# A two-layer attention kernel: loads and means in a new order at its beginning, scores, sums and check in a new order at its end

## The chip, the core and the metric

The kernel runs on one core of a Trainium2 chip. The metric is device time in microseconds (us) from launch to end. The profile names the engines PE (TensorE, matrix products), PEld (its weight loads), DVE (VectorE), ACT (ScalarE), POOL (GpSimd) and SP (SyncE, which issues DMAs); a q behind a name means the engine's sequencer, which waits, branches or issues. L348 is line 348 of the kernel before.

## What is computed

Sixteen images of 256 channels and 32 x 32 positions go through the same layer twice, with other weights each time:

```python
xn = gn(x)                      # 16 groups of 2 columns of h; mean and variance over channels, w and the 2 columns
q, k, v = Wq@xn + bq, Wk@xn + bk, Wv@xn + bv        # 4 heads of 64 channels, n = 1024 positions
rel = (rel_h + rel_w).reshape(heads, d, n)
attn = softmax(q^T k + rel^T q, axis=-1)            # n x n for each head
x = x + v @ attn^T
```

All is float32.

## The kernel before

**Units and blocks.** A unit is one image in one layer; there are 32, and `units` orders them so that an image's second layer comes some units after its first. A unit has two pairs of heads, a pair two halves of 512 output positions; each such half is a block, numbered 0 to 127. A block works over eight groups j of 128 positions of the softmax axis.

**A block.** For each j, `seed` (L327) has VectorE write the position term of the scores into a PSUM tile, as a broadcast sum of two small tables that `positions` (L297) has multiplied out. `scores` (L342) adds the product of k and q to it: four products of 64 x 64 weights and 512 columns, one for each quarter of the array (two row halves are the two heads, two column halves the two parts of j). ACT takes the exponential with a constant shift (L357), and `add_up` (L360) adds the eight results up on VectorE for the softmax sums. `attend` (L372) multiplies the eight results with v. It does so in two stretches, `values_of_p(0)` and `values_of_p(1)`, since the second writes the same PSUM places from the other half of the array's rows: `stretches` (L143) has GpSimd set a one-element tile, `token` (L152), when the first stretch is done, and the second waits for it. The products q, k and v of the next unit, its normalisation and its position tables are spread over the blocks (`prepare`, L472, and the `norm_` functions), and stand on TensorE between the scores. The last unit's blocks 126 and 127 have no such pieces.

**The softmax sums.** In the second block of a pair `sums_of_p` (L395) multiplies the added-up results of both blocks with ones and writes them beside the attention output in the same PSUM tile. `take_out` (L412) has ACT copy both out, and four DMAs lay the sums out over the partitions of `den_all`. Two blocks later `reciprocals` (L435) inverts them (a 128 x 16 form), sends them to DRAM and reads them back broadcast; `finish` (L450) multiplies, adds bias and the image, and in the second layer sends the result out. For the last pair these two steps follow block 127 (L714, L715).

**The check.** The constant shift is right only while all sums lie in a range. After the fast path the kernel compares all 1024 columns of `den_all` with both bounds (L969, L971), takes the minimum (L973), sums it over the partitions with a product (L975) and writes the count to `flag` (L977). All engines read the flag and branch round a slower general path (L979), which these inputs don't take.

**PSUM and order.** The eight banks of PSUM are four tiles of two banks, named a, b, c and d; `ring` says which block step uses which. The order of every engine's work is the order in the source (`manual_schedule`); an engine takes its instructions in that order.

**The beginning.** Lines 603 to 610 issue the loads: image 0, Wq and Wk of layer 0, the small tables of layer 0 (eleven DMAs of positions tables and biases, `load_rest`, L925, on ACT's queue), both Wv, image 1, Wq and Wk of layer 1, image 2, and the tables of layer 1. Eight semaphores serve all DMAs in turn, so a later DMA waits for the landing of an earlier one. `transposed` (L113) turns the weights on TensorE and has ACT copy them out of PSUM. Unit 0 is normalised by special code: `reduced` (L620) sums on VectorE, `first_mean` (L631) averages over partitions with a product, ACT and VectorE share squares and centring, `first_var` (L647) makes variance, reciprocal square root (GpSimd's power, L652) and shift (L654), ACT normalises 5 groups from x and VectorE scales 11. Then come q, k, positions and values of unit 0, and beside them unit 1's centring, squares and variance, on VectorE and GpSimd.

Of the kernel before, what the change touches and what calls it, by code (L numbers as in the profile page):

```python
# [17 lines left out]
P = 128  # L18
# [25 lines left out]
def flat(ap):  # L44
    return ap.rearrange("p w h -> p (w h)")
# [7 lines left out]
def fast_path(ctx, tc, sh, x, layers, out, W, den_all, token):  # L53
# [58 lines left out]

    def transposed(tag, raw, parts):  # L113
        ps = psum2(tag, raw.name + "_t")
        for a in range(2):
            for cc in range(CC):
                for oc in range(CC):
                    nc.tensor.transpose(
                        ps[:, a, cc * C + oc * P : cc * C + (oc + 1) * P],
                        raw[:, a, oc * C + cc * P : oc * C + (cc + 1) * P],  # L120
                        W.ident,
                    )
        for a, (l, part) in enumerate(parts):
            w = {"Wq": W.wq, "Wk": W.wk, "Wv": W.wv}[part][l]
            nc.scalar.copy(w.rearrange("p a c -> p (a c)"), ps[:, a, :])
# [9 lines left out]
    def psum2(tag, name):  # L135
        return ps_s.tile([P, 2, HALF], F32, tag=tag, name=name)
# [205 lines left out]
    def scores(blk, j):  # L342
        u, pr, half = blk
        ps = seeds.pop((blk, j))
        for h, hs in enumerate(QUARTERS):
            for x, c in enumerate(QUARTERS):
                j0 = j * P + x * D
                nc.tensor.matmul(  # L348
                    ps[c, h, :],
                    ks[u, pr][hs, j0 : j0 + D],  # L350
                    qs[u, pr][hs, half * HALF : (half + 1) * HALF],
                    start=False,
                    stop=True,
                    skip_group_check=True,
                )
        p = ppool.tile([P, 2, HALF], F32, tag="p", name=f"p_{u}_{pr}_{half}_{j}")
        nc.scalar.activation(p, ps, AF.Exp, bias=W.shift)  # L357
        probs[blk, j] = p
# [53 lines left out]
    def take_out(blk, po):  # L412

        u, pr, half = blk
        if half == 0:
            outs[u, pr] = opool.tile([P, 3, HALF], F32, tag="od", name=f"od_{u}_{pr}")
            nc.scalar.copy(
                outs[u, pr][:, 0, :].rearrange("p (a n) -> p a n", a=2), po[:, :, :QUART]
            )
            return  # L420
        od = outs[u, pr]
        nc.scalar.copy(  # L422
            od[:, 1:3, :].rearrange("p z (a n) -> p z a n", a=2),
            po.rearrange("p a (z n) -> p z a n", z=2),
        )
        R = P // 4
        n = index[blk]
        for x in range(2):
            for h in range(2):
                r0 = (2 * x + h) * R  # L430
                nc.sync.dma_start(  # L431
                    den_all[h * D : (h + 1) * D, n - 1 + x, :], od[r0 : r0 + 1, 2, :]
                )

    def reciprocals(u, pr):  # L435

        n = index[u, pr, 0]
        r8 = fpool.tile([P, 2, 8], F32, tag="r8", name=f"r8_{u}_{pr}")
        nc.vector.reciprocal(r8, den_all[:, n : n + 2, :])
        rd = dpool.tile([2, 2, HALF], F32, tag="rd", name=f"rd_{u}_{pr}")  # L440
        for x in range(2):
            nc.sync.dma_start(rd[:, x, :].rearrange("h (a b) -> h a b", b=8), r8[:, x, :])
        rdens[u, pr] = opool.tile([P, 2, HALF], F32, tag="rden", name=f"rden_{u}_{pr}")
        for h in range(2):
            nc.sync.dma_start(
                rdens[u, pr][h * D : (h + 1) * D],
                rd[h : h + 1].to_broadcast([D, 2, HALF]),
            )
# [12 lines left out]

    blocks = [(u, pr, half) for u in range(NU) for pr in range(CC) for half in range(NH)]
# [3 lines left out]

    ring = ["b", "c", "a", "d"]
# [30 lines left out]
    def block(n):  # L498
# [7 lines left out]
        pieces = u + 1 < NU or b < 2  # L506
        f0, f1, f2, f3 = ring

# [38 lines left out]
        if pieces and half == 0:  # L547
            ring[2:] = f3, f2
# [52 lines left out]


    load_x(0)
    raw0 = load_raw("raw0", [(0, "Wq"), (0, "Wk")])
    W.load_rest(nc.scalar, 0)
    raw1 = load_raw("raw1", [(0, "Wv"), (1, "Wv")])
    load_x(1)
    raw2 = load_raw("raw2", [(1, "Wq"), (1, "Wk")])
    load_x(2)
# [10 lines left out]
    def reduced(u):  # L620
        red = small.tile([P, CC, G], F32, tag="first_red", name=f"first_red_{u}")
        for cc in range(CC):
            nc.vector.tensor_reduce(
                red[:, cc, :],
                xt[units[u][0]][:, cc, :].rearrange("p (w g t) -> p g w t", g=G, t=GT),
                AX.XY,
                ALU.add,
            )
        return red

    def first_mean(u, pm, red):  # L631
# [15 lines left out]
    def first_var(u, pm, red):  # L647
        nc.tensor.matmul(pm, W.avg, red, start=True, stop=True)
        var = small.tile([P, G], F32, tag="var", name=f"var_{u}")
        nc.vector.tensor_scalar(var, pm, EPS, None, ALU.add)  # L650
        rstd = small.tile([P, G], F32, tag="rstd", name=f"rstd_{u}")
        nc.gpsimd.tensor_tensor(rstd, var, W.mhalf[:, :G], ALU.pow)  # L652
        shift = small.tile([P, G], F32, tag="nshift", name=f"nshift_{u}")
        nc.gpsimd.tensor_tensor(shift, negs[u], rstd, ALU.mult)  # L654
        rss[u] = (rstd, shift)

    G1, G2 = G // 2 + 1, G // 4 + 1
    transposed("a", *raw0)
    transposed("b", *raw1)
    pm0 = psum2("c", "pm_0")  # L660
    first_mean(0, pm0[:, 0, :G], reduced(0))
    norm_squares(0, range(G1))
    centred(0, G1, G)
    sq = ppool.tile([P, 2, HALF], F32, tag="p", name="first_sq_0")
    sq = sq.rearrange("p a n -> p (a n)")[:, : CC * sh.W * (G - G1) * GT].rearrange(
        "p (w g t) -> p w g t", g=G - G1, t=GT
    )
    nc.vector.tensor_tensor(sq, by_group(xns[0], G1), by_group(xns[0], G1), ALU.mult)
    nc.vector.tensor_reduce(
        sums[0][:, G1:], sq.rearrange("p w g t -> p g w t"), AX.XY, ALU.add  # L670
    )
    first_var(0, pm0[:, 1, :G], sums.pop(0))
    transposed("a", *raw2)
    pm1 = psum2("d", "pm_1")
    first_mean(1, pm1[:, 0, :G], reduced(1))
    centred(0, G2, G1)
    norm_apply(0, range(G2))
    nc.vector.tensor_tensor(
        by_group(xns[0], G2), by_group(xns[0], G2), spread(rss[0][0], G2), ALU.mult
    )  # L680
# [9 lines left out]
    centred(1, 0, G)  # L690
    red = small.tile([P, CC, G], F32, tag="first_red", name="first_sums_1")
    for cc in range(CC):
        sq = ppool.tile([P, 2, HALF], F32, tag="p", name=f"first_sq_1{cc}")
        sq = sq.rearrange("p a n -> p (a n)")
        nc.vector.tensor_tensor(sq, xns[1][:, cc, :], xns[1][:, cc, :], ALU.mult)
        nc.vector.tensor_reduce(
            red[:, cc, :], sq.rearrange("p (w g t) -> p g w t", g=G, t=GT), AX.XY, ALU.add
        )
    nc.vector.tensor_tensor(sums[1], red[:, 0, :], red[:, 1, :], ALU.add)
# [3 lines left out]
    first_var(1, pm1[:, 1, :G], sums.pop(1))  # L703
# [7 lines left out]
    seed(blocks[0], 3, ring[0])  # L711
    for n in range(len(blocks)):
        block(n)
    reciprocals(*blocks[-1][:2])  # L714
    finish(*blocks[-1][:2])  # L715

# [226 lines left out]
def kernel(  # L943
# [12 lines left out]
    token = const.tile([1, 1], F32, tag="token", name="token")  # L956
    with tc.manual_schedule():
        W = Weights(tc, sh, layers, const)
        fast_path(tc, sh, x, layers, out, W, den_all, token)


    with ExitStack() as s:
        pool = s.enter_context(tc.tile_pool(name="chk", bufs=1))
        psum = s.enter_context(
            tc.tile_pool(name="chk_ps", bufs=1, space=bass.MemoryType.PSUM)
        )
        flatden = den_all.rearrange("p n e -> p (n e)")
        low = pool.tile([P, nblk * 8], F32, tag="low", name="low")
        nc.vector.tensor_scalar(low, flatden, DEN_LO, None, ALU.is_ge)  # L969
        good = pool.tile([P, nblk * 8], F32, tag="good", name="good")  # L970
        nc.vector.scalar_tensor_tensor(good, flatden, DEN_HI, low, ALU.is_le, ALU.mult)  # L971
        cnt = pool.tile([P, 1], F32, tag="cnt", name="cnt")
        nc.vector.tensor_reduce(cnt, good, AX.X, ALU.min)  # L973
        pc = psum.tile([P, 1], F32, tag="pc", name="pc")
        nc.tensor.matmul(pc[0:1, :], cnt, W.ones[:, 0:1], start=True, stop=True)  # L975
        flag = const.tile([1, 1], I32, tag="flag", name="flag")
        nc.vector.tensor_copy(flag, pc[0:1, :])  # L977
# [33 lines left out]
```

## Time and profile before

| what | value |
|---|---|
| median of 3 runs | 2645.45 us (2643.64 to 2645.61) |
| profiled execution, its own time | 2646.91 us |
| span, first to last instruction | 2643.5 us |
| mean granted TensorE clock | 0.994 |
| busy: PE, PEld, DVE, ACT, POOL | 2589.6, 1394.9, 2422.9, 1979.9, 175.3 us |
| L348, one pass of a score product, 64x512 | 593 ns, 8192 of them |
| L332, one seed, 128x1024 | 1228 ns, 1024 of them |
| L357, one exponential, 128x1024 | 1114 ns |
| L652, GpSimd's power at the beginning | 2.9 us |
| first q product (L251) | starts at 25.91 us |
| last attention product to flag | 2615.2 to 2637.9 us |

A float32 product runs as two passes, and the four quarters of the array work at the same time: the passes of one score group start within 20 ns of each other and the next group's 429 ns later, so a group of four products holds TensorE for 0.86 us. [...] A group of the timeline is a row of start, length, engine, line, operation and count; the rows of the chain are start, length and what; those of the windows give for each engine the busy time and the number of its instructions, then the granted clock (PEclk), the share of the DMA engines and GB/s.

### The profile page before, as it was taken

What the parts mean: (1) busy time and instruction counts of PE and PEld (TensorE: products, weight loads), DVE (VectorE), ACT (ScalarE), POOL (GpSimd) and SP (SyncE); (2) the same over time, 40 slices, a digit from 0 to 9 for tenths busy, and PEclk for the clock granted to TensorE, in tenths of its full rate; (3) what the DMA queues carried; (4) which work ended last, traced back from release to release, by engine and by line L of the source; (5) the groups of instructions that cost most, each with busy time, mean ns of one, the idle gap of its engine ahead of it and who ended that gap; (6) DMA issues with size and microseconds to landing.
All of it is one profiled execution on the core that took longest, in us unless ns stands there. A gap on an engine that the chain in (4) does not pass through costs nothing.

```text
span 2643.5 us, 86127 instructions
## 1 busy us (share of the span) xinstructions
PE 2589.6 (98%) x38406; PEld 1394.9 (53%) x38406; DVE 2422.9 (92%) x2198; ACT 1979.9 (75%) x3916; POOL 175.3 (7%) x450
## 2 busy tenths in 40 slices
PE   7999999999999999999999999999999999999994
PEld 3555555555555555555555555555555555555552
DVE  6999999999999999999999999999999999999996
ACT  5787777787777887777877777877778777778652
POOL 1000000000000000000000000000000000000000
PEclk9999999999999999999999999999999999999997
DMA  2010010100101010010100101001010100100001
GB/s 75 11 34 19 10 50 18 34 26 18 42 19 41 19 42 18 18 50 10 42 26 10 50 18 34 27 16 44 19 34 26 36 25 18 30 14 27 26 26 34
DMA packets 61499, 75.48 MB, mean 29 GB/s; under 512 B 43200, under 2 KB 44736, under 8 KB 61120
## 3 DMA queue, kind: packets, MB, share of 16 engines
q1 hardware_dynamic: 59664, 69.83, 9.0%
q8 instruction: 302, 4.95, 0.8%
q14 instruction: 77, 0.63, 0.1%
q10 hardware_dynamic: 1456, 0.07, 0.0%
HBM read 52.04 MB, written 17.30 MB: 26 GB/s over the span
## 4 chain that ended last, share of the span: by engine, by line
PE 96%; issue 1%; DVE 1%; DMA 1%; POOL 0%; ACT 0%; SPq 0%; DVEq 0%; POOLq 0%
PE po L382 34%; PE ps L348 33%; PE pk L251 8%; PE pv L281 8%; PE pq L251 8%; PE po L405 2%; PE pa L309 2%; PE pm L196 0%; DMA den_all<-od 0%; DVE ps L332 0%; SPq L431 0%; POOL rstd L652 0%; DVE acc L368 0%; ACT od L422 0%; DMA rden<-rd 0%
## 5 line engine op out<-in xcount | busy, mean ns | idle before, releaser
L332 DVE TENSOR_TENSOR ps<-abt 128x1024 f32<-128x1024 f32 x1024 | 1228.7, 1228 | 121.6 <-ACT p L357 103.8
L357 ACT ACTIVATE p<-ps,shift 128x1024 f32<-128x1024 f32 x1024 | 1091.7, 1114 | 325.9 <-PE ps L348 203.8
L348 PE MATMUL ps<-q,k 64*64 64x512 f32 x8192 | 995.5, 593 | 7.4 <-DVE ps L332 7.1
L368 DVE TENSOR_TENSOR acc<-acc,p 128x1024 f32<-128x1024 f32 x768 | 933.6, 1216 | 16.5 <-ACT var L218 0.5
L382 PE MATMUL po<-p,v 64*64 64x256 f32 x16384 | 934.2, 377 | 0.3 <-POOL token L152 0.3
L382 PEld LDWEIGHTS po<-p,v 64*64 64x64 f32 x16384 | 670.0, 133 | 294.6 <-issue 60.9
L348 PEld LDWEIGHTS ps<-q,k 64*64 64x64 f32 x8192 | 301.7, 133 | 427.6 <-issue 281.5
L251 PE MATMUL pq<-xn,Wq 64*64 64x512 f32 x2048 | 244.6, 593 | 4.0 <-ACT xn L231 4.0
L281 PE MATMUL pv<-Wv,xn 64*64 64x256 f32 x4096 | 244.3, 376 | 1.5 <-POOL token L152 1.3
L251 PE MATMUL pk<-xn,Wk 64*64 64x512 f32 x2048 | 244.0, 592 | 0.0
L231 ACT ACTIVATE xn<-x,nshift,rstd 128x128 f32<-128x128 f32 x501 | 213.5, 500 | 1.6 <-POOL nshift L654 1.6
L281 PEld LDWEIGHTS pv<-Wv,xn 64*64 64x64 f32 x4096 | 153.8, 133 | 103.0 <-issue 52.1
L176 ACT ACTIVATE junk<-x,neg 128x128 f32<-128x128 f32 x489 | 191.6, 400 | 0.0
L152 POOL MEMSET token<- 1x1 f32 x380 | 33.5, 88 | 2351.3 <-PE po L382 660.9
L422 ACT COPY od<-po 128x1024 f32<-128x1024 f32 x64 | 64.8, 1012 | 152.2 <-PE po L405 152.2
L366 DVE TENSOR_TENSOR acc<-p,p 128x1024 f32<-128x1024 f32 x128 | 155.9, 1218 | 0.0
L251 PEld LDWEIGHTS pq<-xn,Wq 64*64 64x64 f32 x2048 | 78.6, 134 | 145.7 <-issue 133.1
L176 ACT ACTIVATE junk<-x 128x128 f32<-128x128 f32 x480 | 145.1, 312 | 0.8 <-DVE x L457 0.8
L251 PEld LDWEIGHTS pk<-xn,Wk 64*64 64x64 f32 x2048 | 75.8, 134 | 125.0 <-issue 125.0
L220 POOL TENSOR_TENSOR rstd<-var,mhalf 128x16 f32<-128x16 f32 x30 | 112.3, 3743 | 59.2 <-ACT var L218 59.2
L262 ACT ACTIVATE q<-pq,bq 128x1024 f32<-128x1024 f32 x64 | 71.4, 1116 | 39.4 <-PE pq L251 39.4
L291 ACT COPY v<-pv 128x1024 f32<-128x1024 f32 x64 | 64.8, 1012 | 48.1 <-PE pv L281 48.1
(59 smaller groups left out, 929.2 us busy)
## 6 DMA issues: line engine op xcount, KB each, us to landing
rden<-rd SPq DMA_DIRECT2D x128, 256.0 KB
x<-in_x_dram SPq DMA_DIRECT2D x32, 512.0 KB
out_dram<-x SPq DMA_DIRECT2D x32, 512.0 KB
den_all<-od SPq DMA_DIRECT2D x256, 2.0 KB
rd<-r SPq DMA_DIRECT2D x128, 4.0 KB
raw<-in_L_conv_Wq_dram SPq DMA_DIRECT2D x2, 256.0 KB
raw<-in_L_conv_Wk_dram SPq DMA_DIRECT2D x2, 256.0 KB
raw<-in_L_conv_Wv_dram SPq DMA_DIRECT2D x2, 256.0 KB
```

The costliest lines, as they stand in the source:

```text
L176: nc.scalar.activation(junk, grouped(xt[units[u][0]], g), func, accum_out=into[:, g : g + 1], **bias)
L220: nc.gpsimd.tensor_tensor(rstd, var, W.mhalf[:, :G], ALU.pow)
L231: nc.scalar.activation(grouped(xns[u], g), grouped(xt[units[u][0]], g), AF.Identity, bias=shift[:, g : g + 1], scale=rstd[:, g : g + 1],)
L251: yield nc.tensor.matmul(pk[c, nh, :], w[l][rs, cc, c0 : c0 + D], xns[u][rs, cc, nh * HALF : (nh + 1) * HALF], start=(t == 0 and cc == 0), ...
L262: nc.scalar.activation(t.rearrange("p (a n) -> p a n", a=NH), pk, AF.Identity, bias=bias[l][:, pr : pr + 1])
L281: yield nc.tensor.matmul(pv[c, a, i, :], xns[u][rs, cc, j0 : j0 + D], W.wv[l][rs, cc, :], start=(t == 0 and cc == 0 and i == 0), stop=(t = ...
L332: nc.vector.tensor_tensor(ps.rearrange("p h (w y) -> p h w y", y=H), ab[:, :, :H].unsqueeze(2).to_broadcast([P, 2, XH, H]), ab[:, :, H + h ...
L348: nc.tensor.matmul(ps[c, h, :], ks[u, pr][hs, j0 : j0 + D], qs[u, pr][hs, half * HALF : (half + 1) * HALF], start=False, stop=True, skip_g ...
L357: nc.scalar.activation(p, ps, AF.Exp, bias=W.shift)
L366: nc.vector.tensor_tensor(accs[blk], probs[blk, 0], probs[blk, 1], ALU.add)
L368: nc.vector.tensor_tensor(accs[blk], accs[blk], probs[blk, j], ALU.add)
L382: yield nc.tensor.matmul(po[c, a, :QUART], vts[u][rs, j, c0 : c0 + D], p[rs, h, a * QUART : (a + 1) * QUART], start=(t == 0 and j == 0), s ...
```

## The change

It has two parts, and one change in between.

**Beginning.** The loads come in the order image 0, Wq and Wk of layer 0, image 1, both Wv, Wq and Wk of layer 1, tables of layer 0, image 2, tables of layer 1, all on SP's queue. The means of unit 0 stand ahead of the weight transposes, and those of unit 1 ahead of q. The copies of transposed weights are split off (`taken`). ACT squares 10 groups of unit 0 and VectorE 6; VectorE centres all 16 groups, and both engines scale the centred copy (ACT 4 groups, VectorE 12), so unit 0 has no shift. ACT squares half of unit 1's groups. Unit 1's power comes behind the first values, and its shift is made on VectorE.

**Scores.** In `scores` the loop over the column halves is now outside and that over the row halves inside, for every block.

**End.** Blocks 126 and 127 have a function of their own. Scores 4, 5 and 6 of both have no seed: the position term is a second product, of q with a wide table that VectorE makes in block 125 (`widen`). Seed 7 comes ahead of the others. Block 126's sums are taken in block 127 after scores 3, and their reciprocals are fetched in it. Block 127's sums go to PSUM tiles of their own: as rows that are already spread over the partitions, whose reciprocal VectorE takes directly (128 x 512), and as columns for the check. The last image is finished and sent in halves. The check of the first 992 columns of `den_all` stands in block 126, that of the rest at the end.

```diff
-    W.load_rest(nc.scalar, 0)
+    load_x(1)
     raw1 = load_raw("raw1", [(0, "Wv"), (1, "Wv")])
-    load_x(1)
     raw2 = load_raw("raw2", [(1, "Wq"), (1, "Wk")])
+    W.load_rest(nc.sync, 0)
     load_x(2)
...
+    G1, G2 = G // 2 + 2, G // 4
+    pm0 = psum2("c", "pm_0")
+    for cc in range(CC):
+        reduced(0, cc)
+    first_mean(0, pm0[:, 0, :G])
     transposed("a", *raw0)
+    norm_squares(0, range(G1))
+    centred(0, 0, G)
+    rest_of_squares(0, G1)
+    rstd0 = first_rstd(0, first_var(0, pm0[:, 1, :G]))
+    taken(raw0[1])
     transposed("b", *raw1)
+    taken(raw1[1])
+    pm1 = psum2("d", "pm_1")
+    for cc in range(CC):
+        reduced(1, cc)
+    first_mean(1, pm1[:, 0, :G])
+    transposed("a", *raw2)
+    for g in range(G2):
+        nc.scalar.activation(
+            grouped(xns[0], g), grouped(xns[0], g), AF.Identity, scale=rstd0[:, g : g + 1]
+        )
+    nc.vector.tensor_tensor(
+        by_group(xns[0], G2), by_group(xns[0], G2), spread(rstd0, G2), ALU.mult
+    )
+    taken(raw2[1])
+    norm_squares(1, range(0, G // 2))
+    centred(1, G // 2, G)
+    rest_of_squares(1, G // 2)
...
     seed(blocks[0], 3, ring[0])
+    rstd1 = first_rstd(1, var1)
+    shift1 = small.tile([P, G], F32, tag="nshift", name="nshift_1")
+    nc.vector.tensor_tensor(shift1, negs.pop(1), rstd1, ALU.mult)
+    rss[1] = (rstd1, shift1)
     for n in range(len(blocks)):
         block(n)
-    reciprocals(*blocks[-1][:2])
-    finish(*blocks[-1][:2])
```

```diff
-        for h, hs in enumerate(QUARTERS):
-            for x, c in enumerate(QUARTERS):
+        for x, c in enumerate(QUARTERS):
+            for h, hs in enumerate(QUARTERS):
                 j0 = j * P + x * D
...
+                terms = [(ks[u, pr], qs[u, pr])]
+                if tag:
+                    terms = [(qs[u, pr], wide[u, pr])] + terms
+                for i, (a, b) in enumerate(terms):
...
+    def block_without_pieces(n, half):
+
+        blk = blocks[n]
+        u, pr, _ = blk
+        f0, f1, f2, f3 = ring
+        if half == 1:
+            add_up(blocks[n - 1], 7)
+        for j in range(1, 4):
+            scores(blk, j)
+        if half == 1:
+            po = pos[n - 1]
+            sums_of_p(blocks[n - 1 : n], po)
+            nc.scalar.copy(
+                outs[u, pr][:D, 2, :].rearrange("p (a n) -> p a n", a=2), po[:D, :, QUART:]
+            )
+            keep_sums(outs[u, pr], n - 1, 1)
+        add_up(blk, 1)
+        seed(blk, 7, f2)
+        add_up(blk, 2)
+        reciprocals(*(blocks[n - 2][:2] if half == 0 else (u, pr, 1)))
+        add_up(blk, 3)
+        for j, tag in ((4, f1), (5, f0), (6, f1)):
+            scores(blk, j, tag)
+        scores(blk, 7)
+        add_up(blk, 4)
+        if half == 0:
+            seed(blocks[n + 1], 0, f0)
+        po = pos[n] = psum2(f3, f"po_{n}")
+        values_of_p = attend(blk, po)
+        values_of_p(0)
+        if half == 0:
+            scores(blocks[n + 1], 0)
+        if half == 0:
+            seed(blocks[n + 1], 1, f1)
+            seed(blocks[n + 1], 2, f2)
+        add_up(blk, 5)
+        if half == 0:
+            seed(blocks[n + 1], 3, f0)
+        add_up(blk, 6)
+        if half == 0:
+            finish(*blocks[n - 2][:2])
+            in_range(flatden[:, : 8 * (n - 2)], 0)
+            values_of_p(1)
+            take_out(blk, po)
+            return
+        add_up(blk, 7)
+        acc = accs.pop(blk)
+        pd = psum2(f0, "pd")
+        sums_on_rows(acc, pd)
+        values_of_p(1)
+        finish_half(u, pr, 0, outs[u, pr][:, 0, :], rdens[u, pr][:, 0, :])
+        rden = rdens[u, pr][:, 1, :]
+        nc.vector.reciprocal(rden, pd[:, 0, :])
+        pd = psum2(f2, "pd_columns")[:, 0, : 2 * HALF // P]
+        sums_on_columns(acc, pd)
+        finish_half(u, pr, 1, po[:, :, :QUART], rden)
+        in_range(flatden[:, 8 * (n - 3) : 8 * n], 1)
+        in_range(pd, 2)
+        nc.vector.tensor_reduce(good[:, 3:4], good[:, 0:3], AX.X, ALU.min)
+        pc = psum2(f1, "pc")[0:1, 0, 0:1]
+        nc.tensor.matmul(pc, good[:, 3:4], W.ones[:, 0:1], start=True, stop=True)
+        nc.vector.tensor_copy(flag, pc)
```

`finish_half` is `finish` on 512 columns, `in_range` the two comparisons and the minimum, `sums_on_rows` two products of 64 columns of ones with 512 columns of sums, `sums_on_columns` eight products with 128 columns of sums as weights and one column of ones. `W.load_rest`, `sums_of_p`, `attend` and `seed` are as before.

## The prediction

> **What bounds the kernel now.** I read the chain that ended last first, then its first 70 us and its last 80 us in order of time, then the timeline of both stretches, the windows with the granted clock, and the row of the reciprocal.
>
> ```profile
> PE 96%; issue 1%; DVE 1%; DMA 1%; POOL 0%; ACT 0%; SPq 0%; DVEq 0%; POOLq 0%
> ```
>
> TensorE carries 96% of the span. The rest lies at the two ends. At the beginning:
>
> ```profile
> 19.12 2.92 POOL rstd L652
> ...
> 22.11 1.67 POOL nshift L654
> ...
> 25.91 3.69 PE pq L251 x16
> ...
> 40.38 1.17 POOL nshift L654
> 41.55 0.04 POOL token L152
> ...
> 41.64 1.96 PE pv L281 x32
> ```
>
> The columns are start, length, what. The first real product, q, starts at 25.91, after GpSimd's power and shift. At 40.38 GpSimd is busy with unit 1's shift while TensorE waits for a one-element memset in the same queue. From 41.64 to about 2577 TensorE doesn't stop. At the end:
>
> ```profile
> 2615.20 1.04 PE po L405 x16
> ...
> 2624.87 3.93 DMA rden<-rd
> ...
> 2631.50 2.65 DMA out_dram<-x
> ...
> 2637.78 0.15 DVE flag L977
> ```
>
> The last attention product ends at 2615.2; 22.7 us of sums, DMA round trips, finish, output and check follow until the flag at 2637.9, and a fixed 5.5 us of branch and barriers to 2643.5.
>
> ```profile
> 2581.50:2584.90 3.40, 1.01 (x8) 0.21 (x8) 3.40 (x5) 0.88 (x1) 0.00 (x0) 1.00 0.04 2
> 2584.90:2588.30 3.40, 2.22 (x16) 0.75 (x16) 3.40 (x5) 1.21 (x2) 0.00 (x0) 0.50 0.58 154
> ```
>
> In the last two blocks VectorE is full (3.40 of 3.40) and TensorE busy 1.01: the seeds bound them, and after that stretch the granted clock is 0.50 until 2591.7.
>
> **The beginning, step by step.** Image 0's second half lands at 5.76; its reduce ends at 7.0 now too. Today L633 stands behind 16 weight transposes, so the negative mean comes at 14.55. Afterwards the means are first: 0.71 from reduce to ACT (as 21.28 to 21.99 for unit 1) plus 0.20 gives 7.9. The ACT table load (1.28, now at 8.47 behind eleven small DMA issues) becomes ACT's first instruction and hides under the load of x. Then ACT squares 10 groups at 0.39 (3.59 for 9): 11.9. VectorE centres all 16 groups (2.31, row of the 128x2048 form), squares and sums 6 groups: 768 elements at the slope between 680 ns for 512 and 1091 ns for 896 are 0.96 each. It ends at 12.25, and is the later. Product and variance as now (18.17 to 19.03) 0.86: 13.1. Power on GpSimd with its start 3.0: 16.1. The shift (1.67) leaves the path, because the centred copy is only scaled: VectorE scales 12 groups, 1536 elements, in 1.76: 17.9. ACT's four groups wait for unit 1's mean: VectorE reduces unit 1 in 2.33 behind the variance (15.45), 0.71 to ACT, 0.2, four groups 1.65: 18.0. TensorE does the third pair of transposes behind that mean: 2.0, to 18.15. So three engines meet at 18.1, and q starts at 18.15 instead of 25.91: **7.75 us**.
>
> Moved on SP: image 1 ahead of Wv, and eleven small tables from ACT's queue to SP's, ahead of image 2 and layer 1's tables. In the trace a DMA waits for the semaphore of an earlier one (Wq is issued at 4.33, when x lands); the changed program's first eight loads have none. About 3.5 MB at the 350 to 400 GB/s of the busy microseconds is 9 to 10 us: weights by about 13, needed at 12.9 (Wv) and 16.1. The tables, 0.6 us an issue, land by about 17; q's bias is first read near 26, rel near 28. Image 2 lands near 21 instead of 19, first read about 37. All this costs nothing under the chain above; if Wv were 2 us late, ACT's copies would push its scaling by about as much.
>
> Unit 1's shift goes to VectorE, and its power behind the token. q, k, positions and values keep their lengths (q start to first scores), but the second stretch of values starts when scores 0 end, 40.2 instead of 41.64: **1.45 us**. The power's reader, the first normalisation in block 0, comes seven microseconds later. The clock: q's weight loads step 0.85 us until 31.7 and 0.43 after, so TensorE ran at half for 5.8 us. The Trainium skill ("TensorE: Matmul & The Clock Gate", Part 1) has a free-running window of 3.4 us that must be busy, which makes this 3.4 to 6.8, less if the transposes that now run up to q count. Half of the difference is the gain: -0.5 to 2.9; I take **0.7**. Beginning: 9.9, from 8 to 12.
>
> **The middle.** `scores` now loops over columns outside and rows inside, in all 1024 groups of four products. No row has this order. A changed order next to products in the old one could cost one or two dispatch slots, the 6.5 ns by which the four starts of a group lie apart, at some ten changes in each of 126 blocks: 8 to 16 us, and the skill's Part 3 of that page says so: matmuls start and end strictly in program order.
>
> ```profile
> 1002.94 0.65 PE L348 MATMUL ps<-q,k 64*64 64x512 f32 x2
> 1002.95 0.21 PE L196 MATMUL pm<-sum,avg 64*64 64x16 f32 x2
> 1003.01 1.05 PE L348 MATMUL ps<-q,k 64*64 64x512 f32 x6
> ```
>
> But here a pair of scores starts before the second pass of the mean that stands ahead of it, and the other pair 0.07 later: each quarter of the array follows its own queue. By the rule 8 to 16 us, by the row **0**, both ends: the four start within 20 ns and stream 429 ns, and the last in either order is the same quarter, so nothing is gained. I take 0.
>
> **The end.** `widen` (one 1.22 us add) enters block 125 ahead of a seed that ended 0.48 before TensorE took it: VectorE is back to back there, the seed comes 1.02 late, TensorE stalls **0.6**. Block 126: six seeds in two blocks are replaced by a second term of the scores, 0.86 us of TensorE each, saving 1.13 of VectorE. Times without the 0.6: scores 1 to 3 end 2579.1; 4, 5, 6 at 1.72 and 7 at 0.86: 2585.1 (their exps, 1.11, are done in time); values 3.45, score 0.86, values 3.45: 2592.9, where before it was 2598.4. VectorE in the meantime: from 2578.8 three adds and seed 7, reciprocal, four seeds, two adds (1.13 unchained, 1.26 chained) to 2593.1, then finish 2.5, the check of 992 old sums 3.1 (0.70 + 1.23 + 1.22 now), the last add 1.2: 2599.8. Queued on TensorE behind that add are the sums of block 126, and behind them block 127's scores 4: TensorE is done with scores 3 at 2595.5 and **waits 4.3 us**. The windows above say what follows: 2.4 us idle in one brought half clock for 6.8 us. I charge 1.8 (0.8 of about 2.2).
>
> Then: sums 1.05, copy 0.6, two DMAs 2.35: reciprocal at 2604.0 (VectorE waits 0.75); five chained adds to 2610.6; TensorE's scores 4 to 7 and values, 9.5 us, end 2610.4. Sums on rows 0.95, values 3.5: 2615.15. Half 0's reciprocals arrive by DMA (6.9 after 2604.25) at 2611.2, its finish takes 1.35. Then a reciprocal of 512 elements.
>
> ```profile
> L439 DVE RECIPROCAL r<-den_all x64: 252/253/255, 88.7 to 2621.0; 128x16 f32<-128x16 f32 x64
> ```
>
> A 16-element scalar op takes 173 ns, of which 156 are fixed; the reciprocal 253, so 6.1 ns an element: 512 make 3.3 us. The skill ("VectorE: DVE Perf Modes", "First, the fixed hardware budget") says the divide repeats 8 times, at 0.96 GHz 8.3 ns: 4.4; and if the extra were fixed, 0.75. I take the row's 3.3: 2615.95, so it ends behind the values and is on the path. Finish of half 1 1.35; two small checks (3 ops of 0.2 each) and the minimum 1.45; product and flag 0.55: 2619.3. The eight column sums (16 weight loads of 0.11 to 0.21) end before the second check. The output's 2.65 lies beside this and the 5.5 us of the exit, where SP collects the DMA semaphores. With 0.6 and 1.8 the flag comes at 2621.7 instead of 2637.9: **16.2**, from 13.5 to 19.5.
>
> **Sum.** 9.9 + 16.2 = 26.1. The profiled execution had 2643.5 of span in 2646.9; it lies 1.5 above the median 2645.45. Carried to the median: 2619.35, I say 2619.5.
>
> **Rivals.** (A) As worked out, 0.85, 2613 to 2626: 2613 if the clock warms early, doesn't drop, and the reciprocal is short. (B) The two terms of a quarter hold up the other quarters, so that a double score runs on two quarters at a time: 3.44 instead of 1.72, six times 1.72 is 10.3: 2630. For it: no row has two products in one quarter in succession; against: at 1002.94 products passed five pending ones in each of two quarters. 0.08. (C) Slower: the loop order costs. Place: each of 1024 score groups; price: one exposed weight load, 55 ns from a quarter's first to its second load when a group starts after idle, so 56 us: 2675. It decides from 26.1/1024 = 25 ns a group. Against it: the weight loads of the next group start with the matmuls of this one. 0.05. (D) Nothing is won because waits close up again within 0.2% (5 us, about what a measurement can tell): would need both ends to fail, 0.02.
>
> The range 2613 to 2627 holds most of A and the cheap side of B, about 8 in 10.
>
> **What would show it.** q's first product near 18, values' second stretch near 32 without a power ahead; the same busy time per score group (593 ns a pass); a TensorE gap of about 4 us near the end before L431's sums, with the check of 992 sums beside it on VectorE, and clock 0.5 behind it; a reciprocal 128x512 of about 3 us; flag 3 to 5 us after the last values. Wrong if score passes lengthen, if Wv or image 1 lands after 14, or if the double scores take over 2 us.

## The result, and the profile after

| | before | after |
|---|---|---|
| median of 6 runs | 2645.44 us (2643.64 to 2647.76) | 2619.13 us (2617.52 to 2619.93) |
| ratio of the runs | | 0.9901, 95% interval 0.9888 to 0.9913 |
| profiled execution, its own time | 2646.91 us | 2619.18 us |
| span | 2643.5 us | 2617.6 us |
| flag written | 2637.93 us | 2610.04 us |
| one pass of a score product | 593 ns | 592 ns |

The kernel became 26.3 us faster; 26.1 were forecast (2619.5). The share of TensorE in the chain that ended last, from the page of after:

```profile
PE 97%; DVE 1%; DMA 1%; SPq 0%; issue 0%; ACT 0%; POOL 0%; DVEq 0%
```

TensorE now carries 97% instead of 96%: less stands at the two ends. The beginning of that chain in order of time:

```profile
13.11 2.92 POOL rstd L798
...
16.05 1.77 DVE xn L825
...
17.96 3.11 PE pq L257 x16
...
29.70 1.01 PE ps L374 x8
30.71 1.73 PE pv L287 x32
32.44 2.57 PE ps L374 x24
```

The power is followed directly by the scaling, with no shift between, and q starts at 17.96 instead of 25.91. At 29.70 scores 0, at 30.71 the second stretch of values, with nothing of GpSimd between them; before, GpSimd's shift and the token stood there. The scores behind the values come at 32.44; the chain of before has them at 43.60:

```profile
43.60 2.58 PE ps L348 x24
```

So **11.16 us** are won by then. The end of the chain of after:

```profile
2587.85 1.15 DVE acc L394
...
2589.13 1.92 PE po L431 x8
2591.05 7.76 PE ps L374 x56
2598.81 3.45 PE po L408 x64
2602.26 1.01 PE pd L509 x4
2603.27 3.66 PE po L408 x64
...
2606.96 0.70 DVE od L495
...
2609.89 0.15 DVE flag L734
```

Between the last values and the flag there are 3.1 us, before 22.7. The sums of block 126 (L431) stand behind the last add of that block (L394) and take 1.92 us, where the same products take 1.06 at full clock (in `gap_filled` below). The windows show why:

```profile
2585.40:2588.80 3.40, 0.00 (x0) 0.00 (x0) 3.33 (x4) 0.89 (x1) 0.00 (x0) 0.76 0.38 154
2588.80:2592.20 3.40, 3.07 (x16) 1.23 (x20) 3.40 (x4) 0.58 (x1) 0.00 (x0) 0.50 0.00 0
```

TensorE does nothing for a whole window while VectorE is full (finish and the check of 992 sums), and the clock is 0.50 after it. The wait is 4.29 us long. The long reciprocal, as the trace's group of that line:

```profile
L725 DVE RECIPROCAL rden<-pd x1: 3358/3358/3358, 2603.3 to 2603.3; 128x512 f32<-128x512 f32 x1
```

It takes 3.36 us (6.3 ns an element beside the fixed part) and ends at 2606.68, a quarter of a microsecond ahead of the last values.

In the profiled executions the gain splits like this. The rows of the blocks are read at the first exponential of a block.

| stretch | before | after | won |
|---|---|---|---|
| start to q | 25.91 | 17.96 | 7.95 |
| q to the first exponential | 14.52 | 12.81 | 1.71 |
| from there to the scores behind the values | 3.17 | 1.67 | 1.50 |
| from there to block 125 | 2510.41 | 2510.20 | 0.21 |
| block 125 to the flag | 83.92 | 67.40 | 16.52 |
| flag to the end of the span | 5.53 | 7.58 | -2.05 |
| sum | | | 25.84 |

The loss from the flag to the end of the span is not seen in the own times of these two executions. They differ by 27.73 us and not by 25.84, since what lies outside the span fell from 3.4 to 1.6 us.

### The profile page after: what moved, and what is told of

It is laid out like the page before. It is cut to its first block, busy times and chain, and to the rows that moved or that the text cites. A ratio compares the mean times of both kernels' runs of the same rounds, so it can differ in the third digit from the quotient of the medians.

```text
span 2617.6 us, 86262 instructions
## 1 busy us (share of the span) xinstructions
PE 2593.7 (99%) x38466; PEld 1404.4 (54%) x38466; DVE 2419.0 (92%) x2200; ACT 1982.8 (76%) x3933; POOL 173.1 (7%) x448
## 4 chain that ended last, share of the span: by engine, by line
PE 97%; DVE 1%; DMA 1%; SPq 0%; issue 0%; ACT 0%; POOL 0%; DVEq 0%
PE ps L374 34%; PE po L408 33%; PE pk L257 8%; PE pq L257 8%; PE pv L287 8%; PE po L431 2%; PE pa L315 2%; PE pm L202 0%; DVE acc L394 0%; DMA den_all<-od 0%; DVE ps L338 0%; SPq L459 0%; DMA x<-in_x_dram 0%; DMA rden<-rd 0%; ACT od L448 0%
## 5 line engine op out<-in xcount | busy, mean ns | idle before, releaser
L394 DVE TENSOR_TENSOR acc<-acc,p 128x1024 f32<-128x1024 f32 x768 | 934.1, 1216 | 18.1 <-ACT p L383 1.4
```

The costliest lines, as they stand in the source:

```text
L394: nc.vector.tensor_tensor(accs[blk], accs[blk], probs[blk, j], ALU.add)
```

## The experiments

The twelve runs below stand in three groups, each beside runs of the kernel before on the same chip (medians there 2646.4, 2646.4 and 2645.2). All medians are of four or five runs; the 95% interval of a ratio is about 0.0015 to each side, 4 us. Differences of two or three microseconds between variants are therefore read from the traces, and the medians only have to agree.

### One end at a time

`begin_only` is the kernel before with the new beginning; `end_only` is the kernel after with the old beginning.

```diff
 # begin_only, against the kernel before
-    W.load_rest(nc.scalar, 0)
+    load_x(1)
...
+    first_mean(0, pm0[:, 0, :G])
     transposed("a", *raw0)
...
 # end_only, against the kernel after
-    load_x(1)
+    W.load_rest(nc.scalar, 0)
...
     transposed("a", *raw0)
+    transposed("b", *raw1)
+    pm0 = psum2("c", "pm_0")
+    first_mean(0, pm0[:, 0, :G], reduced(0))
```

> The kernel before with only the new beginning (loads, means, transposes, unit 1's power); old loop order, old end. Theory (the two ends add up, and the beginning is worth what stands at the first scores of the profile after, 43.60 - 32.44 = 11.2 us): 2634.2 us (2633 to 2635.5), q near 18.0, block 126 starts 11.2 earlier than before, and the time from the last attention product to the flag is 22.7 us as before. Rival (part of the gain at the beginning is eaten later in this kernel and only shows because the new end takes it up, or belongs to the loop order): 2637 or more. The prediction's own term was 9.9 us: 2635.5.

> The kernel after with the old beginning. Theory (the ends add up): 26.3 - 11.2 = 15.1 us from the end, 2630.3 us (2629 to 2631.5); q at 25.9, and from the start of block 126 the same times as in the kernel after: flag 44.5 us after it. The prediction's own term for the end was 16.2: 2629.2. Rival (the clock windows fall elsewhere against the work, since the start is later by another 11 us): up to 3 us either way in the last 40 us.

Measured: `begin_only` 2633.46 us (ratio 0.9951, 0.9938 to 0.9965), 13.0 won; `end_only` 2628.05 (0.9930, 0.9917 to 0.9944), 18.4 won. Together 31.4, some 5 more than both ends give in one kernel. The order of the stretches in their traces tells where this lies. At block 124 `begin_only` is 11.87 us ahead of before, as expected, but it also takes 20.99 us from block 126 to block 127, where the kernel before takes 23.06, though both run the same code there. Windows of `begin_only`:

```profile
2570.00:2573.40 3.40, 1.39 (x8) 0.21 (x8) 3.40 (x4) 0.51 (x1) 0.00 (x0) 0.83 0.04 2
2573.40:2576.80 3.40, 2.95 (x24) 0.88 (x24) 3.40 (x4) 1.81 (x2) 0.00 (x0) 0.67 0.61 159
```

Half speed begins in both kernels just behind a pause of TensorE of 2.69 us. Here it lasts 3.41 us (2572.24 to 2575.65, TensorE busy for 2.96 of them), in before 6.83 (2584.87 to 2591.70, TensorE busy for only 2.23 of the first 3.41). In all fourteen traces the recorded changes of the granted clock lie whole multiples of 3.41 us apart, and the pause ends 0.23 us ahead of such a change here and 0.98 ahead of it in before. So the same code is 2 us faster. The new end takes this pause out anyway, so these 2 us are counted twice in the sum.

At the flag `begin_only` is 13.74 us ahead of before, `end_only` 17.40 and after 27.89, so the sum is 3.25 too large there: 1.87 of it is this half clock, and the rest lies in steps of under 0.5 (`end_only` wins 16.93 us from block 124 to the flag, after 16.51). The medians alone don't settle it, since each of the three ratios has an interval of some 4 us to either side. As far as the traces show, the ends add up in work; in time the clock's phase is in between.

### After once more, and the loop order

```diff
 # old_order, in scores
-        for x, c in enumerate(QUARTERS):
-            for h, hs in enumerate(QUARTERS):
+        for h, hs in enumerate(QUARTERS):
+            for x, c in enumerate(QUARTERS):
```

> The kernel after, unchanged, beside the others of this call. The two ends alone gave 13.0 and 18.4 us, 31.4 together, 5 more than the 26.3 of both. Theory (the sum was flattered: with the new beginning alone the half clock of block 126 stayed away, 2.0 us that the new end takes out as well, and the profile of after had a last VectorE instruction 2.3 us late): 26.3 again, some 2619.5 us, and a span within 1 us of 2617.6 or, if the late instruction was chance, 2 us less. Rival (the ends add up and the first measurement was high): 2615 us.

> The kernel after with the old loop order in all scores (row halves outside, column halves inside), the double ones too. Theory (each quarter follows its own queue): no difference from after in blocks 0 to 125, within 0.3 us from the exponential of block 32 to that of block 124 (1849.7 us), and double scores at 1.72 to 1.75 us. Rival (program order costs 6.5 to 13 ns a group): 7 to 13 us of difference. Rival 2 (the order matters for double scores alone, where the second column half then waits for two products): 0.4 us for each of six.

Measured: after again 2618.80 us (0.9899), with the flag at 2609.21 and the span's end 6.25 later. So 27.6 against the runs of before beside it and 26.3 in the first measurement, both below 31.4, though the intervals are too wide for these medians to show that the ends don't add up. From flag to the span's end the fourteen profiled executions took 5.3 to 7.6 us, before 5.53 and the first of after 7.58. In thirteen of them all engines but VectorE are done after 5.3 to 5.7, and only VectorE's last semaphore instruction comes later, in after by 2.3; what delays it, no run shows. Between before and after the own times don't show it: beside the stretch from the span's start to the flag they have 8.98 us in before and 9.14 in the first of after (7.3 to 9.2 in the fourteen).

`old_order` took 2618.98 us (0.9899), 0.2 more than the runs of after beside it. From block 32 to block 124 it needs 1848.82 us, after 1849.69 and 1848.88 in its two executions, before 1850.03: the order of the loops costs nothing, neither in the 1024 groups nor for the double scores (block 126 takes 17.64 us in either order).

### The wait ahead of the sums of block 126

`add7_early` moves one add ahead of finish and check, so that TensorE needn't wait for these.

```diff
-        if half == 1:
-            add_up(blocks[n - 1], 7)
         for j in range(1, 4):
             scores(blk, j)
...
         add_up(blk, 6)
         if half == 0:
+            add_up(blk, 7)
             finish(*blocks[n - 2][:2])
             in_range(flatden[:, : 8 * (n - 2)], 0)
```

> The kernel after with the last add of block 126 ahead of finish and the check of 992 sums, so that TensorE does not wait 4.3 us for it ahead of the sums. Theory 1 (VectorE's sum of work bounds the tail; the gap is only where it shows): VectorE still has finish 2.5 and check 3.1 ahead of block 127's adds, its last add comes at most 2.7 us earlier, TensorE waits some 3.3 us later, ahead of the sums on rows: 2616.4 us (2615.5 to 2618). Theory 2 (the prediction's charge: 4.3 us of gap and 1.8 us of half clock are paid on the path): 6 us less, 2613. Theory 3 (the second gap halves the clock ahead of the last values, 3.5 us of TensorE work): nothing won, 2619.

Measured: 2616.42 us (0.9885, 0.9870 to 0.9900). The gap of 4.29 is gone, and another one has come. Timeline of `add7_early` (in brackets the idle time before and what ended it):

```profile
2599.51 1.08 PE L509 MATMUL pd<-acc,ones 128*64 128x512 f32 x4 [3.33 <-DVE acc L394]
...
2600.52 5.37 PE L408 MATMUL po<-p,v 64*64 64x256 f32 x64
```

TensorE waits 3.33 us for the last add of block 127, and its last values take 5.37 instead of 3.66, partly at half clock. The last add of block 127 ended 38.0 us after the first exponential of block 126, against 40.6 and 39.6 in after. That is theory 1, with some of theory 3: VectorE's sum of work bounds the tail, and the gap is only where it shows.

### Taking the check off VectorE

Two kernels take the 3.1 us of the check away from VectorE, on top of `add7_early`. `check_pool_add7` has GpSimd compare and ACT sum up; `act_check` has ACT do both, with Relu of the distance to each bound and its sum, which must be zero.

```diff
 # check_pool_add7
+        nc.gpsimd.tensor_scalar(t, den, DEN_LO, None, ALU.is_ge)
+        nc.gpsimd.tensor_scalar(s, den, DEN_HI, None, ALU.is_le)
+        nc.gpsimd.tensor_tensor(t, t, s, ALU.mult)
...
-            in_range(flatden[:, : 8 * (n - 2)], 0)
             values_of_p(1)
+            beside.append(in_range_beside(flatden[:, : 8 * (n - 2)]))
...
 # act_check
         values_of_p(0)
         if half == 0:
+            beside.extend(out_of_range(flatden[:, : 8 * (n - 2)]))
             scores(blocks[n + 1], 0)
...
-            in_range(flatden[:, : 8 * (n - 2)], 0)
...
+        for i, (scale, edge) in enumerate(((-1.0, DEN_LO), (1.0, -DEN_HI))):
+            e = small.tile([P, 1], F32, tag=f"edge{i}", name=f"edge{i}")
+            nc.gpsimd.memset(e, edge)
...
+            nc.scalar.activation(
+                two[:, i, : den.shape[-1]], den, AF.Relu, bias=e, scale=scale, accum_out=side
+            )
```

> As add7_early, and the check of the 992 old sums is made by GpSimd (two comparisons and a product), with their count summed up by ACT, so that VectorE has 3.1 us less. Theory 1 (VectorE's sum of work bounds the tail): last add near 2596 instead of 2601.8, no TensorE gap over 1 us and no half clock in block 127; then half 0's reciprocals (7.3 us by DMA) and the reciprocal of 512 elements, 3.4 us, end behind the values: flag 4.3 us earlier, 2614.8 us (2613.5 to 2616.5). Theory 2 (the gap alone): 2613, no difference from add7_early. Rival 3: GpSimd's reads beside VectorE's adds slow them: adds over 1.3 us each while it works, and half of the gain lost.

> As add7_early, with the check of the 992 old sums made by ACT as two Relu passes with a sum each, in the pause of ACT beside the first values of block 126, so that VectorE has 3.1 us less and GpSimd reads nothing beside it. Theory (VectorE's sum of work bounds the tail): last add near 2595.5 to 2596.5 instead of 2599.4, TensorE's wait ahead of the sums on rows under 1 us instead of 3.3, no half clock in the last values, which then take 3.7 instead of 5.4: flag near 2604, 5 us less than in add7_early, 2611.5 us (2610.5 to 2613.5). Rival (ACT's two passes delay the exponentials of block 127's first scores and TensorE waits for them): 1 to 2.5 us of this lost.

Measured: `check_pool_add7` 2618.02 us (0.9892), nothing better than `add7_early`. Its timeline:

```profile
2582.19 3.17 DVE L394 TENSOR_TENSOR acc<-acc,p 128x1024 f32<-128x1024 f32 x2
2582.34 3.62 POOL L511 TENSOR_SCALAR range<-den_all 128x992 f32<-128x992 f32 x1
...
2586.04 2.61 POOL L512 TENSOR_TENSOR range<-range 128x992 f32<-128x992 f32 x1
...
2586.53 3.20 DVE L485 SCALAR_TENSOR_TENSOR x<-od,bv,x 128x1024 f32<-128x1024 f32 x1
```

Two adds take 3.17 us together, where they take 2.48 in `add7_early`, and finish's second step takes 3.20, where it takes 1.28 elsewhere: 2.6 of the 3.1 us saved are lost while GpSimd works beside them, and the last add comes only 0.4 earlier than in `add7_early`. So rival 3 is right in kind and more than half of the gain is gone. The Trainium skill ("SBUF — State Buffer", section "Who interferes with whom") says that a VectorE instruction with two inputs in SBUF contends with a GpSimd instruction that reads SBUF; both slowed rows have two such inputs, and there the trace agrees. Not every such instruction is slowed, though: the first of the two adds took 1.22, and a seed beside the first comparison its usual 1.23.

`act_check`: **2612.47 us** (0.9873, 0.9858 to 0.9888), 6.3 less than the runs of after beside it, the fastest of all.

```profile
2586.24 1.11 PE L374 MATMUL ps<-wide,q 64*64 64x512 f32 x8
...
2587.15 1.06 PE L374 MATMUL ps<-q,k 64*64 64x512 f32 x8
...
2588.01 1.10 PE L374 MATMUL ps<-wide,q 64*64 64x512 f32 x8
...
2588.87 1.10 PE L374 MATMUL ps<-q,k 64*64 64x512 f32 x8
...
2596.76 1.08 PE L523 MATMUL pd<-acc,ones 128*64 128x512 f32 x4 [0.72 <-DVE acc L394]
...
2597.77 3.68 PE L408 MATMUL po<-p,v 64*64 64x256 f32 x64
```

TensorE's second wait shrinks from 3.33 to 0.72 us, its clock stays at 1.00 through block 127, and the values are back at 3.68. The last add ends 34.9 us after the first exponential of block 126, 3.0 earlier than in `add7_early`, just the 3.1 taken from VectorE. The first scores of block 127 start at the same place after it as in `add7_early`: ACT's two passes fit into its pause. Theory 1 stands, theory 2 (only the gap matters) is out.

### The seeds kept

```diff
-            scores(blk, j, tag)
+            seed(blk, j, tag)
+            scores(blk, j)
...
-        if u + 1 == NU and b == 1:
-            widen(u, 1)
```

> The kernel after with seeds for scores 4, 5 and 6 of the last two blocks as before, no double scores and no wide table. Theory (VectorE's sum of work bounds the tail): six seeds more are 6.8 us of VectorE, of which some 2.5 fit in its pauses, while 5.2 us of TensorE work are saved for nothing; 0.4 to 0.8 us of the wide table come back: flag 3 to 5 us later, 2623.5 us (2622 to 2625.5). Rival (the double scores cost TensorE as much as they save VectorE): no difference, 2619. Rival 2 (TensorE bounds): 4 us less, 2615.

Measured: 2631.75 us (0.9945, 0.9932 to 0.9959), 13.0 more than the runs of after beside it, three times what was expected. Its timeline:

```profile
2573.84 3.37 PE L374 MATMUL ps<-q,k 64*64 64x512 f32 x16 [5.66 <-DVE ps L338]
...
2602.54 3.69 PE L374 MATMUL ps<-q,k 64*64 64x512 f32 x16 [5.65 <-DVE ps L338]
```

In both blocks TensorE waits 5.7 us for the first of the three seeds, and then runs at half clock. I had counted VectorE's six seeds as work to be added up, but in this order they stand behind three adds, seed 7 and a reciprocal, so TensorE is idle until they are through. So the run is no clean price of a seed: in `begin_only`, where the seeds stand in their old places, block 126 takes 20.99 us against 23.64 here and 17.64 in after. It does tell that the double scores don't cost TensorE what they save VectorE, and that they let TensorE run on past VectorE's queue. From block 124 to 126 this kernel takes 39.96 us, like before and `begin_only`, and after 40.41: that is the wide table, 0.45 us (0.32 to 0.83 in all the kernels that have it).

### The clock: the idle window filled, and a warm start

`gap_filled` gives TensorE nine products of no use in the wait of 4.29 us; `warm` gives it two at the beginning, where it is idle.

```diff
 # gap_filled, in block 127
+            for i in range(9):
+                nc.tensor.matmul(
+                    po[:, i % 2, QUART:], W.ident, ks[u, pr][:, :QUART],
+                    start=True, stop=True, skip_group_check=True,
+                )
             sums_of_p(blocks[n - 1 : n], po)
...
 # warm
     transposed("a", *raw0)
+    warm = psum2("d", "warm")
+    for c0, c1 in ((0, HALF), (HALF // 2, HALF)):
+        nc.tensor.matmul(warm[:, 0, c0:c1], W.ident, raw0[0][:, 0, c0:c1], start=True, stop=True)
```

> The kernel after with nine products of no use (identity times 256 columns of k) in the 4.3 us for which TensorE waits ahead of the sums of block 126. This takes the idle window away and leaves the wait. Theory (the half clock is due to the idle window, and VectorE bounds the tail): the clock stays at 1.00, the sums take 1.06 instead of 1.92, VectorE's reciprocal comes 0.9 earlier (2593.2) and so does the flag; 2618.2 us. The prediction's charge for the half clock was 1.8: 2617.3. Rival (the clock halves all the same, or the products of no use cost more than the idle time): no difference or later.

> The kernel after with two products of no use (the identity with 512 and with 256 columns of raw weights) behind the first weight transposes, where TensorE is idle from 9.3 to 12.2. Theory (busy time ahead of q warms the clock, transposes and products alike; that is why q ran at half speed for 2.5 us and not for 5.8): the weight loads of q step by 0.43 us from its start, half of 2.5 us is gained ahead of the first scores: first exponential near 29.7 instead of 30.5 to 31.5, 2617.6 us (0.8 to 1.5 less than after). Rival (only what runs right ahead of q counts): q as in after, no difference. Rival 2 (the two products run past 12.2 and delay the variance): up to 1 us more.

`gap_filled`: 2616.58 us (0.9891), 2.2 to 2.6 less than the two medians of after. Timeline:

```profile
2589.73 1.06 PE L431 MATMUL po<-acc,ones 128*32 128x256 f32 x8
```

Windows:

```profile
2585.40:2588.80 3.40, 3.40 (x19) 2.97 (x16) 3.33 (x5) 1.59 (x2) 0.00 (x0) 1.00 0.38 154
2588.80:2592.20 3.40, 3.29 (x28) 1.47 (x27) 3.40 (x4) 0.58 (x1) 0.00 (x0) 1.00 0.00 0
```

The sums start as long after block 126's beginning as in after, the clock stays at 1.00, the sums take 1.06 instead of 1.92. The flag comes 46.6 us after the first exponential of block 126, in after 48.8 and 47.9. VectorE gains 0.95 at its reciprocal, as expected, and against the first execution of after another 1.0 by the last add, because its five adds now follow each other without waiting for exponentials of slow scores; I had left that out. In the second execution of after the adds hardly wait. The half clock lasts 6.83 us in the first and 3.41 in the second, and costs 2.3 and 1.4 us.

`warm`: 2618.89 us (0.9899), no gain. The windows of `warm`:

```profile
11.90:15.40 3.50, 1.94 (x15) 1.63 (x15) 2.65 (x4) 1.97 (x4) 2.45 (x1) 1.00 0.29 36
15.40:18.80 3.40, 2.69 (x18) 1.74 (x21) 2.89 (x2) 3.09 (x11) 0.46 (x1) 0.55 0.59 147
```

The clock did rise: the second group of transposes takes 1.07 us, where it takes 1.95 in after. But with these faster transposes TensorE is busy for only 1.94 of 3.50 us, the clock falls to 0.55, and q runs at half for 5.0 us instead of 2.5. Cut where the recorded clock changes, it is full from 12.31 to 15.72, with TensorE busy for 2.18 of these 3.41 us, and half from there to 22.55. The theory was half right (busy time ahead of q counts). That the cure failed because warm work fills the time less fits these numbers; no run tests it by itself. The Trainium skill ("TensorE: Matmul & The Clock Gate", Part 1, "HAM oscillation") gives as its rule to leave TensorE no gap of more than some 3.4 us; here the longest gap ahead of q was 0.71 us and the clock fell all the same, so keeping to that rule was not enough.

### The power on GpSimd

```diff
     var1 = first_var(1, pm1[:, 1, :G])
+    rstd1 = first_rstd(1, var1)
+    shift1 = small.tile([P, G], F32, tag="nshift", name="nshift_1")
+    nc.gpsimd.tensor_tensor(shift1, negs.pop(1), rstd1, ALU.mult)
+    rss[1] = (rstd1, shift1)
```

(and the power, with VectorE's shift, taken away behind the first values)

> The kernel after with unit 1's power and shift on GpSimd right behind the variance, ahead of the first values' token, as they stood before. Theory (the queue of GpSimd holds up the token, prediction's term 1.45 us): power from 27.7 for 2.9, shift 1.2, token near 31.9 instead of 29.9, second stretch of values near 32.0 instead of 30.1; scores 1 some 1.5 us later (33.9 instead of 32.4); 2620.5 us. Rival (TensorE has scores 0 to do and the rest closes up in block 0): the second stretch is late, but the start of block 1 isn't, 2619.

Measured: 2619.32 us (0.9902). Timeline:

```profile
30.77 1.16 POOL L847 TENSOR_TENSOR nshift<-neg,rstd 128x16 f32<-128x16 f32 x1
...
31.87 0.09 POOL L158 MEMSET token<- 1x1 f32 x1
32.01 1.96 PE L287 MATMUL pv<-Wv,xn 64*64 64x256 f32 x32 [1.28 <-POOL token L158]
```

The second stretch starts at 32.01, as expected; the scores behind it come at 33.79 instead of 32.26, 1.53 later, and ten microseconds on the row of two score groups that stands at 43.43 in after stands at 44.97: nothing closes up in block 0. At block 124 it is 1.0 to 1.2 behind after. The medians, 0.2 to 0.5 apart, are too coarse to show it.

### Both together

> act_check and warm together, as the best version. If both gains stand: 2612.5 - 1.2 = 2611.3 us, first exponential near 29.8 and flag near 2604. If warm gives nothing: 2612.5.

Its edit is that of `act_check` and that of `warm`. Measured: 2613.23 us (0.9879, 0.9863 to 0.9895). `warm` gives nothing here either; q runs at half clock for 6.0 us. `act_check` alone is the version to keep, 33.9 us below the runs of before beside it.

## Why the prediction was right, point by point

- **q from 25.91 to 18.15 (7.75 us).** Right: 17.96, 7.95 won. The power starts at 13.11 (13.1 worked out), and the scaling ends at 17.82. The transposes of Wv start at 12.65, so weights and tables behind them on SP's queue held nothing up. Of the 7.95 us, 6.01 are won when the power starts (13.11 instead of 19.12, with the means first and the squares shared anew) and 1.94 behind it (with no shift and a new split of the scaling). No run takes these parts from each other; the chain shows them one behind the other.
- **Second stretch of values (1.45).** Right: 1.50, and `power_shift` gives 1.53 back.
- **The clock ahead of q (0.7, from -0.5 to 2.9).** The sign was right and the size too small: 1.71 in the profiled execution, where q's weight loads step by 0.85 us until 20.45 instead of 31.8. (The record of the granted clock has its first entry, at full speed, at 20.36 in after and 31.70 in before; the 1.00 that the windows print ahead of it says nothing.) But the term is no constant: over ten executions with this beginning (without `warm`) q was slow for 0.9 to 4.1 us, median 2.5. The two of after alone had 2.5 and 4.1. At half speed that is 1.6 us of time between executions of one and the same beginning.
- **The beginning (9.9, 8 to 12):** 11.16, nearly all of the difference being the clock.
- **The loop order (0).** Right, by the row and by `old_order`; the rule of program order would have asked for 8 to 16 us.
- **`widen` (0.6).** 0.45 us.
- **The wait ahead of block 126's sums (4.3).** Right: 4.29. Its price was not: `add7_early`, which takes the gap alone away, is 2.4 to 2.7 us below the two medians of after, and its flag, counted from block 126, comes only 0.3 to 1.2 earlier, since VectorE's work, which caused the gap, is still there.
- **Half clock after it (1.8).** 1.4 to 2.3 by `gap_filled`.
- **The reciprocal (3.3, on the path by 0.8).** The duration was right (3.36, by the slope of the row; 4.4, estimated from the page's eight repeats, and 0.75 are both out). Its place was wrong by a little: it ended 0.25 ahead of the values, since the values themselves ended some 0.9 later than worked out, so it cost nothing.
- **Last values to flag (3 to 5).** 3.1.
- **The end (16.2):** 16.5 from block 125 to the flag.
- **The exit (5.5, taken as fixed).** In the span it is 7.6 in this execution and 5.3 to 7.6 over all; in the own times the two executions are even (8.98 and 9.14 us beside the stretch to the flag).
- **The sum (26.1).** At the flag 27.89 us are won, 1.8 more than forecast: 1.3 in the beginning, 0.2 in the middle, 0.3 at the end. The medians are only 26.3 apart, since the profiled execution of before, from which the terms were read, lies 1.5 us above its median and that of after less than 0.1. So it is luck that the sum is right to 0.2 us; the half speed ahead of q alone moves an execution by up to 1.6.
- **Rival B** (double scores on two quarters at a time) fell: in `act_check` the wide and the k terms of the double scores follow each other every 0.86 us, so a double score is 1.72 us. **Rival C** fell with `old_order`. **Rival D** fell with the result.

## What to carry to other kernels

A gap on the engine that bounds a kernel shows where another engine's queue is too long, and not what is to be won: moving one instruction past the gap gave back under 3 of some 6 us and made a second gap, and taking 3.1 us of work from the late engine gave another 4. Work for the last blocks belongs on an engine that pauses there and doesn't slow the busy engine meanwhile: the same check cost VectorE 2.6 of its 3.1 us when GpSimd did it, and only two operations of 0.15 us at the end when ACT did it. Do a part at a time with a trace of each, since the times of parts need not add up: the same block ran at half clock for 3.41 us in one kernel and for 6.83 in another.

## What the runs showed that I had not expected

- One and the same code in block 126 cost 23.06 and 20.99 us, with half clock for 6.83 and for 3.41 us behind the same pause of 2.69 us.
- TensorE at full clock lost it again ahead of q after a window in which it was busy for 1.94 of 3.50 us, with no gap over 0.71 us.
- While GpSimd worked beside it, one VectorE instruction took 3.20 us instead of 1.28.
- From the flag to the end of the span the same branch and barriers took 5.3 to 7.6 us in fourteen executions, and in all but one (`seeds_kept`, where all engines are late) nearly all of the difference is VectorE's last semaphore instruction. Before and after lie 2.05 us apart by this, and 0.16 in what their own times have beside the stretch to the flag.
